# Row terms of the second layer over DRAM, tangent weights and shorter routing in a fused graph-attention and mixture-of-experts kernel

## The chip, the cores and the metric

The kernel runs on one core of a Trainium2 chip. A core has a matrix engine (TensorE, PE in the profile; its weight loads are listed apart as PEld), a vector engine (VectorE, DVE), an activation engine (ScalarE, ACT), a general engine (GpSimd, POOL) and a synchronisation engine (SyncE, SP) that in this kernel only issues transfers. Each engine executes its own list of instructions strictly in order, and the engines wait for one another through semaphores. Transfers between DRAM and the on-chip memory are issued from SP, ACT or POOL and carried by 16 DMA engines. The metric is the device time of one execution in microseconds.

## The reference

`x` is 64 batches of 256 rows of 256 floats, and `adj` is one 256 x 256 mask that all batches share. All arithmetic is float32. Two layers follow each other; cut to what matters:

```python
x = x + gat4(layernorm(x), adj)            # 4 heads of 64
x = x + layernorm(x) @ weight.T + bias
x = x + gat1(layernorm(x), adj)            # 1 head of 256, slope 0.01, then relu
x = x + moe(layernorm(x))                  # returns its tokens plus the experts' sum

# gat1: h = inp @ W; e[i, j] = leaky_relu(h[i] @ a1 + h[j] @ a2), -1e9 where adj == 0
#       softmax over j, times h
# moe:  logits = tokens @ router_w.T; probs = softmax(logits); the two largest of 8,
#       renormalised to a sum of 1; each expert is gelu(t @ w1 + b1) @ w2 + b2
```

Attention is computed per batch: every row `i` gets a term `h[i] @ a1`, every row `j` a term `h[j] @ a2`, and the score matrix is made from their sum. In the mixture each of the 16,384 tokens goes to two of the eight experts. With two weights that sum to one, a token's weights depend only on the difference `ed` of its second and first logit.

## The kernel before

**Attention.** One batch is 256 rows, two tiles of 128 rows (`NT = 2`). The exponential of a leaky ReLU of a sum is a maximum of two products of exponentials, so the kernel takes exponentials of the terms alone and builds a transposed score tile as `max(row term, bound) * masked factor` with one DVE instruction per tile of 128 x 256. The row terms, one number for each attention row, must then stand along the free dimension, the same on all 128 partitions.

There are two ways to bring them there. For the four heads of the first layer, `send_terms` (L535) turns them on DVE, SP (ACT before batch 18) writes them to a scratch in DRAM (L623), and a second transfer, `spread_terms` (L554, issued at L556), reads that scratch into every partition of the tile `z`. For the single head of the second layer, `scores1` (L522) lets PE do it: for each of the two row tiles a transpose of a broadcast column (L525) puts the terms into a PSUM bank `pd`, and the two instructions of L530 read them from there. `projected1` (L499) makes the exponentials `ex` on ACT (L513), the scaled values (L514) and the masked factor `me` (L519). `attended` (L578) multiplies scores and values (L586) and takes reciprocals of the row sums (L593).

**Routing.** The batches are routed in chunks: eleven of four batches, seven of two and three of one, 61 in all; the last three batches are computed dense, with all experts on all rows. `route` (L1079) finds the two best experts of every token (`top_two`, L783), counts tokens with two matmuls (L1105 and L1106), accumulates over the row tiles with a scan (L1116 for chunks of four; otherwise eight scans at L1122), and sends each row with its row number and weights to a position in the DRAM list `xs` by scattered transfers of POOL (`send`, L1059, issued at L1061). The weights come from the exponential of `ed` on ACT (L1112) and four DVE instructions (`two_weights`, L810). `route_dense` (L1190) does the same for a dense batch, with its exponential at L1195.

**Experts.** The list is worked off in "pairs" of 256 rows of one expert. `expert_pair` (L877) loads rows and first-layer weights (L893, L904, L922), `hidden` (L951) and `result` (L977) multiply, and `scatter` (L985) adds the 256 results to the output with two transfers of POOL that add in DRAM (L991). Each pair's two adds wait until the two adds of the pair before have landed, as different pairs can hold the same output row. The last routed chunk fills up partly filled pairs with filling rows (L1171) whose weights give zero. A filling row needs an output row to be added to: `fill` (L303 to L309) names rows of the last batch, `B - 1`.

That batch is dense, and its own output is a plain store. `store_dense` (L1030) therefore holds the store of batch 63 back until every scatter has been issued, and makes it wait for the last two adds. At the start, `fill_spare` (L313) stores zeros to the output rows of that batch, and the first scatter waits for it.

**Order.** Python generators stand for jobs. In each step of a loop (from L1242) the active jobs run in order of the rank they yielded last; a positive rank ends a job's share of the step, a negative one only re-sorts it inside the step. A batch starts every third step (`TICKS = 3`). What the generators call in this order is the order of the instructions on each engine; the loop knows no durations. `batch_layers` (L596) is a batch's job.

Of the kernel before, what the change touches and what calls it, by code (L numbers as in the profile page):

```python
# [9 lines left out]
F32 = mybir.dt.float32  # L10
# [5 lines left out]
P = 128  # L16
# [11 lines left out]
def kernel(  # L28
# [251 lines left out]
    def pack_expert(e):  # L280
# [22 lines left out]
    fill = const.tile([P, 2, ROW], F32, tag="fill", name="fill")  # L303
    nc.gpsimd.memset(fill, 0.0)
    nc.gpsimd.iota(
        fill[:, :, D : D + 1].bitcast(I32), pattern=[[1, 2], [1, 1]], base=(B - 1) * N,
        channel_multiplier=2,
    )
    nc.vector.memset(fill[:, :, D + 1 : D + 2], -1.0)  # L309
# [3 lines left out]
    def fill_spare():  # L313
        nc.sync.dma_start(
            out=xs_d[E * CAP * PAIR :, :].rearrange("(p t) c -> p t c", t=2), in_=fill
        )
        d = nc.sync.dma_start(
            out=out_rows[(B - 1) * N :, :].rearrange("(p t) c -> p t c", t=2), in_=fill[:, :, :D]
        )
        tc.add_to_no_dep_group("out", d.ins)  # L320
        based.append(d.ins)
        yield 90

    def once(work):
# [30 lines left out]
    scan_mask = const.tile([P, E, NTC], F32, tag="scan_mask", name="scan_mask")  # L355
    nc.vector.memset(scan_mask, 1.0)
    nc.vector.memset(scan_mask[:, :, 0:1], 0.0)

# [163 lines left out]
    def scores1(ex, me):  # L522
        pd = bank("pd", [N])
        for t in range(NT):
            nc.tensor.transpose(  # L525
                pd[:, t * P : (t + 1) * P], ex[:, t, 1:2].to_broadcast([P, P]), ident
            )
        z = work.tile([P, NT, N], F32, tag="z1", name="z1", bufs=1)
        for j in range(NT):
            nc.vector.scalar_tensor_tensor(  # L530
                z[:, j, :], pd, ex[:, j, 2:3], me[:, j, :], op0=ALU.max, op1=ALU.mult
            )
        return [z[:, j, :] for j in range(NT)]

# [61 lines left out]
    def batch_layers(b, c0, xng, lg):  # L596
# [81 lines left out]
        xT = transposed(x2)  # L678
        yield 20
        q, ex, me = projected1(xT, rstd, b)  # L680
        yield 25
        z = scores1(ex, me)
        yield 40
        pvs, rinv = attended(
            q[:, :, None, :], 1, lambda j, h, t: z[j][:, t * P : (t + 1) * P]
# [97 lines left out]
    def top_two(c, nt, lg, first):  # L783


        rt = lambda shape, name: chunk_tile(shape, name, c)
        vec, tt = nc.vector, nc.vector.tensor_tensor
        emb = em8[:, None, :].to_broadcast([P, nt, E])
        ohs, tops, lcur = rt([2, nt, E], "ohs"), [], lg
        for k in range(2):  # L790
            top = rt([nt], f"top{k}")
            vec.tensor_reduce(top, lcur, AX.X, ALU.max)
            eq = rt([nt, E], "eq")
            tt(eq, lcur, top[:, :, None].to_broadcast([P, nt, E]), ALU.is_equal)
# [12 lines left out]
        tt(ed, tops[1], tops[0], ALU.subtract)  # L807
        yield ohs, ed

    def two_weights(less, second, ed):  # L810

        nc.vector.tensor_scalar(less, ed, 1.0, None, op0=ALU.add)
        nc.vector.reciprocal(less, less)
        nc.vector.tensor_tensor(second, ed, less, ALU.mult)
        nc.vector.tensor_tensor(less, less, second, ALU.subtract)

    rows = [keep.tile([P, E], F32, tag="rows", name="rows")]  # L820
    nc.vector.tensor_scalar(rows[0], region, float(PAIR), None, op0=ALU.mult)
# [208 lines left out]
    def store_dense(b):  # L1030

        own = dense_batch[b]
        yield 99
        while b == B - 1 and (scatters or len(added) < 2 * PAIRS):
            yield 99
        d = nc.sync.dma_start(
            out=out_rows[b * N : (b + 1) * N, :].rearrange("(t p) d -> p t d", p=P),
            in_=own["base"],
        )
        before = added[-2:] + based if b == B - 1 else []  # L1040
        tc.declare_no_dep(
            d.ins, query=SYNC, group="out", keep=before,
            reason="no row is added to here, or every add is in their chain",
        )
        for ins in before:
            tc.add_manual_dep(d.ins, ins.name, AFTER, reason="filling rows were added here")
        tc.add_to_no_dep_group("out", d.ins)
        nc.sync.nop()

# [29 lines left out]
    def route(c, row0, nt, n, last, xng, lg):  # L1079
# [29 lines left out]
        both = rt([2, E, nt], "both")  # L1109
        vec.tensor_copy(both, pp)  # L1110
        pre, tot = both[:, 0], both[:, 1]
        nc.scalar.activation(ed, ed, AF.Exp)  # L1112
        tt(tot[:, :, 0], tot[:, :, 0], rows[0], ALU.add)
        run = rt([E, nt], "run")
        if nt == NTC:
            vec.tensor_tensor_scan(  # L1116
                run.rearrange("p e t -> p (e t)"), scan_mask.rearrange("p e t -> p (e t)"),
                tot.rearrange("p e t -> p (e t)"), 0.0, ALU.mult, ALU.add,
            )
        else:  # L1120
            for e in range(E):
                vec.tensor_tensor_scan(  # L1122
                    run[:, e, :], ones[:, :nt], tot[:, e, :], 0.0, ALU.mult, ALU.add
                )
        rows[0] = run[:, :, nt - 1]
        tt(pre, pre, run, ALU.add)
        if spread:
# [8 lines left out]
        vec.tensor_copy(pos, posf)  # L1136
        if not spread:
            yield from later(90, 1, 2)
        two_weights(tail[:, :, 1], tail[:, :, 2], ed)
        for i, xe in enumerate(xng):  # L1140
            vec.tensor_copy(xe[:, :, D + 1 :], tail[:, i * NT : (i + 1) * NT, :])
        parts = allot(c, n, False)
# [69 lines left out]
    PAIRS = ROUTED * NT + E - 1  # L1212

    def jobs():
        b = done = taken = 0
# [104 lines left out]
```

## Time and profile before

The three timed runs gave 1497.18, 1497.51 and 1500.99 us. The profile is of another execution, which took 1509.41 us.

| quantity | value |
|---|---|
| median of three runs | 1497.51 us |
| profiled execution | 1509.41 us, span 1507.6 us |
| PE busy, weight loads busy | 1429.0 us (95%), 1263.9 us (84%) |
| DVE busy | 1252.7 us (83%) |
| ACT busy | 1024.6 us (68%) |
| POOL busy | 870.2 us (58%) |
| transpose of row terms, second layer (L525) | 128, 278 ns mean |
| scores, second layer (L530) | 128, 460 ns mean |
| activation table loads, all lines | 130, 1283 ns each |
| adds to the output (L991) | 258, 1605 ns mean, idle before them 206.6 us |

A group's row gives source line, engine, operation, output and inputs, count, busy time, mean duration of one, and the engine's idle time just before. Durations of matmuls overlap[...]: what a matmul takes from its successors is the distance between starts. The table-load count is the sum of the groups of that operation: 65 before the gelu of L961, 47 before L513, 8 before L1112, 6 before L647, 3 before L1195 and 1 at L235.

### The profile page before, as it was taken

How to read it: one execution, taken by the hardware profiler on the slowest of the kernel's cores; microseconds unless marked ns; L12 is line 12 of the kernel's file. 1: busy time of each engine (PE TensorE's matmuls, PEld its weight loads, DVE VectorE, ACT ScalarE, POOL GpSimd, SP SyncE). 2: the span in 40 equal slices, each digit the busy share in tenths (PEclk: the TensorE clock that was granted, in tenths of full speed). 3: DMA queues.
4: the chain of work that ended last, by engine and by line, in shares of the span. 5: the costliest groups of instructions: out<-in, count | busy, mean ns of one | idle time of the engine just before them, and what ended most of it. 6: DMA issues, size and time to landing. Idle time of an engine off the chain costs nothing. (4 is left out here: it accounts for less than half of the span.)

```text
span 1507.6 us, 30029 instructions
## 1 busy us (share of the span) xinstructions
PE 1429.0 (95%) x8138; PEld 1263.9 (84%) x8138; DVE 1252.7 (83%) x4476; ACT 1024.6 (68%) x2403; POOL 870.2 (58%) x845
## 2 busy tenths in 40 slices
PE   6899999999999999999999999999999999879996
PEld 5788888889898998988998989888888887658885
DVE  7699999888898888889898988998888888765543
ACT  1477667577777777777777787667777878764331
POOL 2122536355867576666758585776666667643444
PEclk9899999899999999999999999999999999999999
DMA  4732334556877777877877677768777775887843
GB/s 134 241 97 67 117 104 131 155 149 142 196 172 190 157 183 155 177 177 180 187 157 183 151 186 164 181 164 187 179 167 170 153 170 124 192 180 161 156 83 50
DMA packets 354354, 236.37 MB, mean 157 GB/s; under 512 B 246276, under 2 KB 316428, under 8 KB 354188
## 3 DMA queue, kind: packets, MB, share of 16 engines
q1 hardware_dynamic: 301272, 158.16, 41.3%
q0 software_dynamic: 48864, 66.33, 23.8%
q10 hardware_dynamic: 4052, 9.98, 2.2%
q8 instruction: 67, 1.10, 0.3%
q14 instruction: 99, 0.81, 0.2%
HBM read 146.00 MB, written 88.35 MB: 155 GB/s over the span
## 5 line engine op out<-in xcount | busy, mean ns | idle before, releaser
L991 POOL DMA_INDIRECT out_dram<-y,xt x258 | 414.1, 1605 | 206.6 <-issue 71.5
L586 PE MATMUL pv<-q,z 128*128 128x65 f32 (+1 forms) x2560 | 365.9, 298 | 0.4
L586 PEld LDWEIGHTS pv<-q,z 128*128 128x128 f32 x2560 | 333.0, 194 | 13.1 <-DVE z L572 1.1
L1061 POOL DMA_INDIRECT xs<-xng,pos x244 | 259.5, 1064 | 65.3 <-issue 60.3
L970 PE MATMUL py<-w2s,hT 128*128 (+1 forms) x1224 | 283.5, 382 | 11.5 <-ACT hT L961 10.3
L970 PEld LDWEIGHTS py<-w2s,hT 128*128 128x128 f32 x1224 | 229.1, 191 | 45.4 <-ACT hT L961 14.2
L955 PE MATMUL ph<-sT,we 128*128 128x256 f32 x1032 | 241.9, 383 | 4.5 <-DVE y L980 2.9
L572 DVE SCALAR_TENSOR_TENSOR z<-z,q,mask 128x256 f32<-128x256 f32 x504 | 231.6, 482 | 15.5 <-DMA z<-terms 6.6
L955 PEld LDWEIGHTS ph<-sT,we 128*128 128x128 f32 x1032 | 195.6, 192 | 32.4 <-DVE y L980 3.6
L461 ACT COPY xT<-pt 128x512 f32<-128x512 f32 x209 | 121.4, 588 | 105.0 <-PE pt L455 72.2
L948 ACT ACTIVATE y<-y,w 128x256 f32<-128x256 f32 x258 | 113.2, 498 | 115.3 <-DVE y L980 100.9
L961 ACT ACTIVATE hT<-ph,we 128x256 f32<-128x256 f32 x306 | 124.1, 472 | 63.5 <-PE ph L955 46.3
L408 POOL TENSOR_SCALAR rstd<-mv 128x4 f32<-128x4 f32 (+1 forms) x66 | 15.6, 236 | 239.4 <-DVE mv L381 184.4
L506 PE MATMUL pq<-wx,xT 128*128 128x259 f32 x512 | 128.8, 394 | 18.6 <-ACT xT L461 16.9
L426 ACT ACTIVATE off<-x,sums 128x256 f32<-128x256 f32 x256 | 129.3, 505 | 8.4 <-DVE x L669 1.6
L506 PEld LDWEIGHTS pq<-wx,xT 128*128 128x128 f32 x512 | 95.6, 193 | 42.6 <-ACT xT L461 25.6
L471 PE MATMUL pq<-wx,xT 128*128 128x268 f32 x512 | 127.1, 391 | 2.8 <-DVE xT L117 1.6
L980 DVE TENSOR_TENSOR y<-py,b2s 128x512 f32<-128x512 f32 x129 | 85.7, 685 | 50.0 <-PE py L970 37.3
L662 PE MATMUL pf<-wfT,xT 128*128 128x256 f32 x512 | 123.8, 385 | 0.0
L471 PEld LDWEIGHTS pq<-wx,xT 128*128 128x128 f32 x512 | 97.5, 191 | 21.9 <-DVE xT L117 1.8
L690 ACT ACTIVATE rel<-pv,rinv 128x256 f32<-128x256 f32 x128 | 54.0, 469 | 76.4 <-DVE rinv L593 52.2
L662 PEld LDWEIGHTS pf<-wfT,xT 128*128 128x128 f32 x512 | 94.7, 195 | 10.8
(174 smaller groups left out, 2400.8 us busy)
## 6 DMA issues: line engine op xcount, KB each, us to landing
we<-wpack SPq DMA_DIRECT2D x145, 288.0 KB
xr<-xs SPq DMA_DIRECT2D x516, 64.0 KB
z<-terms SPq DMA_DIRECT2D x46, 512.0 KB
xin<-in_x_dram SPq DMA_DIRECT2D x64, 256.0 KB
out_dram<-base SPq DMA_DIRECT2D x61, 256.0 KB
xblk<-in_x_dram SPq DMA_DIRECT2D x188, 64.0 KB
z<-terms ACTq DMA_DIRECT2D x17, 512.0 KB
out_dram<-y,xt POOLq DMA_INDIRECT x258
```

What stands on the lines that cost most here:

```text
L426: nc.scalar.activation(off, src[:, t, :], AF.Square, bias=sums[:, t : t + 1], scale=-float(D), accum_out=sq[:, at + t : at + t + 1],)
L461: nc.scalar.copy(dst, pt)
L471: nc.tensor.matmul(pq.rearrange("p h c -> p (h c)"), xT[:, k, t * P : (t + 1) * P], wx[:, k, :], start=(k == 0), stop=(k == KT - 1),)
L506: nc.tensor.matmul(pq, xT[:, k, t * P : (t + 1) * P], wx1[:, k, :], start=(k == 0), stop=(k == KT - 1),)
L572: nc.vector.scalar_tensor_tensor(z[:, j, :, h, :], terms, q[:, j, h, HD + 2 : HD + 3], masks[0][:, j, :].rearrange("p (t i) -> p t i", t=N ...
L586: nc.tensor.matmul(pv[:, h, :], z(j, h, t), q[:, j, h, : d + 1], start=(j == 0), stop=(j == NT - 1),)
L662: nc.tensor.matmul(pf[:, t, :], xT[:, k, t * P : (t + 1) * P], wfT[:, k, :], start=(k == 0), stop=(k == KT - 1),)
L955: nc.tensor.matmul(ph[:, f, :], we[:, k * D + f * P : k * D + (f + 1) * P], xT[:, k, :], start=(k == 0), stop=(k == KT - 1),)
L961: nc.scalar.activation(hT[:, f, :], ph[:, f, :], AF.Gelu, bias=we[:, C_B1 + f : C_B1 + f + 1])
L970: nc.tensor.matmul(py[:, t, :], hT[:, f, t * P : (t + 1) * P], w2s[:, e, f * D : (f + 1) * D].rearrange("p e c -> p (e c)"), start=(f == 0 ...
L991: d = nc.gpsimd.indirect_dma_start(out=out_rows, out_offset=bass.IndirectOffsetOnAxis(ap=xt[:, t, 0:1].bitcast(I32), axis=0), in_=y[:, t, ...
L1061: d = nc.gpsimd.indirect_dma_start(out=xs_d[: E * CAP * PAIR, :], out_offset=bass.IndirectOffsetOnAxis(ap=at, axis=0), in_=xe, in_offset=None,
```

## The change

There are four edits, and one that follows from them.

Firstly, from batch 18 on (`SETTLED`), the second layer's row terms go over DRAM as those of the first layer do. `send_terms1` writes 256 numbers with a transfer from SP; a second one, after the first has landed, reads them into all partitions of the part of `z1` that the last score instruction writes. The transposes and the PSUM bank are left out there. `z1` is allocated before that transfer, and has one buffer as before.

Secondly, the two weights are written with a tangent: their difference is `tanh(-ed / 2)`, and the second is half of one minus it. One ACT instruction and one DVE instruction take the place of one and four. The chunk's activation uses `Tanh` where it used `Exp`.

Thirdly, chunks of one batch and the dense batches find their two experts with the eight-maximum instruction and its index instruction, one of each for each row tile, and chunks of one and two batches use one masked scan in place of eight. Their masks are set on POOL at the start.

Fourthly, filling rows name the rows of the first batch. The zeros at the start and the hold on the last batch's store are left out.

```diff
-        fill[:, :, D : D + 1].bitcast(I32), pattern=[[1, 2], [1, 1]], base=(B - 1) * N,
+        fill[:, :, D : D + 1].bitcast(I32), pattern=[[1, 2], [1, 1]], base=0,
...
-        d = nc.sync.dma_start(
-            out=out_rows[(B - 1) * N :, :].rearrange("(p t) c -> p t c", t=2), in_=fill[:, :, :D]
-        )
-        tc.add_to_no_dep_group("out", d.ins)
-        based.append(d.ins)
...
+    def send_terms1(ex, b):
+
+        ud = tc.dram_tile([N], F32, name=f"terms1_{b}")
+        nc.sync.dma_start(out=ud.rearrange("(t p) -> p t", p=P), in_=ex[:, :, 1])
+        return ud
+
+    def scores1(ex, me, z, spread):
+
+        terms = z[:, NT - 1, :]
+        if not spread:
+            terms = bank("pd", [N])
+            for t in range(NT):
+                nc.tensor.transpose(
+                    terms[:, t * P : (t + 1) * P], ex[:, t, 1:2].to_broadcast([P, P]), ident
+                )
         for j in range(NT):
             nc.vector.scalar_tensor_tensor(
-                z[:, j, :], pd, ex[:, j, 2:3], me[:, j, :], op0=ALU.max, op1=ALU.mult
+                z[:, j, :], terms, ex[:, j, 2:3], me[:, j, :], op0=ALU.max, op1=ALU.mult
             )
...
-        yield 25
-        z = scores1(ex, me)
+        spread = b >= SETTLED
+        if spread:
+            yield -22
+            ud = send_terms1(ex, b)
+            yield -52
+        z = work.tile([P, NT, N], F32, tag="z1", name="z1", bufs=1)
+        if spread:
+            nc.sync.dma_start(out=z[:, NT - 1, :], in_=rows_to_all(ud, N))
+        yield 45 if spread else 25
+        z = scores1(ex, me, z, spread)
...
+        if nt == NT:
+            yield top_two_of_few(c, nt, lg, first)
+            return
...
-    def two_weights(less, second, ed):
-
-        nc.vector.tensor_scalar(less, ed, 1.0, None, op0=ALU.add)
-        nc.vector.reciprocal(less, less)
-        nc.vector.tensor_tensor(second, ed, less, ALU.mult)
-        nc.vector.tensor_tensor(less, less, second, ALU.subtract)
+    def top_two_of_few(c, nt, lg, first):
+
+        top = chunk_tile([nt, E], "eq", c)
+        at = chunk_tile([nt, E], "l2", c, dt=mybir.dt.uint32)
+        for t in range(nt):
+            nc.vector.max(top[:, t, :], lg[:, t, :])
+            nc.vector.max_index(at[:, t, :], top[:, t, :], lg[:, t, :])
+        ohs = chunk_tile([2, nt, E], "ohs", c)
+        for k in range(2):
+            nc.vector.tensor_tensor(
+                ohs[:, k], jrow[:, None, :E].to_broadcast([P, nt, E]),
+                at[:, :, k : k + 1].to_broadcast([P, nt, E]), ALU.is_equal,
+            )
+        nc.vector.tensor_scalar(first, at[:, :, 0], float(-E), None, op0=ALU.add)
+        ed = chunk_tile([nt], "ed", c)
+        nc.vector.tensor_tensor(ed, top[:, :, 1], top[:, :, 0], ALU.subtract)
+        return ohs, ed
+
+    def second_weight(second, less):
+
+        nc.vector.tensor_scalar(second, less, -0.5, 0.5, op0=ALU.mult, op1=ALU.add)
...
-        while b == B - 1 and (scatters or len(added) < 2 * PAIRS):
-            yield 99
...
-        before = added[-2:] + based if b == B - 1 else []
...
-        nc.scalar.activation(ed, ed, AF.Exp)
+        nc.scalar.activation(tail[:, :, 1], ed, AF.Tanh, scale=-0.5)
...
-        if nt == NTC:
-            vec.tensor_tensor_scan(
-                run.rearrange("p e t -> p (e t)"), scan_mask.rearrange("p e t -> p (e t)"),
-                tot.rearrange("p e t -> p (e t)"), 0.0, ALU.mult, ALU.add,
-            )
-        else:
-            for e in range(E):
-                vec.tensor_tensor_scan(
-                    run[:, e, :], ones[:, :nt], tot[:, e, :], 0.0, ALU.mult, ALU.add
-                )
+        vec.tensor_tensor_scan(
+            run.rearrange("p e t -> p (e t)"), scan_masks[nt].rearrange("p e t -> p (e t)"),
+            tot.rearrange("p e t -> p (e t)"), 0.0, ALU.mult, ALU.add,
+        )
...
-        two_weights(tail[:, :, 1], tail[:, :, 2], ed)
+        second_weight(tail[:, :, 2], tail[:, :, 1])
...
-        nc.scalar.activation(ed, ed, AF.Exp)
         two = chunk_tile([2, NT], "two", c)
-        two_weights(two[:, 0], two[:, 1], ed)
+        nc.scalar.activation(two[:, 0], ed, AF.Tanh, scale=-0.5)
+        second_weight(two[:, 1], two[:, 0])
```

More of the change, by code (lines that the diff above doesn't have):

```diff
@@ L354 @@
     region = iota([E], [[CAP, E]], 0, 0, "region")
-    scan_mask = const.tile([P, E, NTC], F32, tag="scan_mask", name="scan_mask")
-    nc.vector.memset(scan_mask, 1.0)
-    nc.vector.memset(scan_mask[:, :, 0:1], 0.0)
+    scan_masks = {}
+    for nt in sorted({nb * NT for nb in CHUNKS}):
+        m = const.tile([P, E, nt], F32, tag=f"scan_mask{nt}", name=f"scan_mask{nt}")
+        nc.gpsimd.memset(m, 1.0)
+        nc.gpsimd.memset(m[:, :, 0:1], 0.0)
+        scan_masks[nt] = m
     half_done = []
@@ L520, in projected1 @@
         return q, ex, me
[L522 to L526, printed above, removed]
-            )
-        z = work.tile([P, NT, N], F32, tag="z1", name="z1", bufs=1)
+    def send_terms1(ex, b):
[10 more added lines that the diff above has]
+                )
         for j in range(NT):
             nc.vector.scalar_tensor_tensor(
-                z[:, j, :], pd, ex[:, j, 2:3], me[:, j, :], op0=ALU.max, op1=ALU.mult
+                z[:, j, :], terms, ex[:, j, 2:3], me[:, j, :], op0=ALU.max, op1=ALU.mult
             )
@@ L1039, in store_dense @@
         )
-        before = added[-2:] + based if b == B - 1 else []
-        tc.declare_no_dep(
-            d.ins, query=SYNC, group="out", keep=before,
-            reason="no row is added to here, or every add is in their chain",
-        )
-        for ins in before:
-            tc.add_manual_dep(d.ins, ins.name, AFTER, reason="filling rows were added here")
+        tc.declare_no_dep(d.ins, query=SYNC, group="out", reason="no row is added to here")
         tc.add_to_no_dep_group("out", d.ins)
@@ L1111, in route @@
         pre, tot = both[:, 0], both[:, 1]
-        nc.scalar.activation(ed, ed, AF.Exp)
+        nc.scalar.activation(tail[:, :, 1], ed, AF.Tanh, scale=-0.5)
         tt(tot[:, :, 0], tot[:, :, 0], rows[0], ALU.add)
         run = rt([E, nt], "run")
-        if nt == NTC:
-            vec.tensor_tensor_scan(
-                run.rearrange("p e t -> p (e t)"), scan_mask.rearrange("p e t -> p (e t)"),
-                tot.rearrange("p e t -> p (e t)"), 0.0, ALU.mult, ALU.add,
-            )
-        else:
-            for e in range(E):
-                vec.tensor_tensor_scan(
-                    run[:, e, :], ones[:, :nt], tot[:, e, :], 0.0, ALU.mult, ALU.add
-                )
+        vec.tensor_tensor_scan(
+            run.rearrange("p e t -> p (e t)"), scan_masks[nt].rearrange("p e t -> p (e t)"),
+            tot.rearrange("p e t -> p (e t)"), 0.0, ALU.mult, ALU.add,
+        )
         rows[0] = run[:, :, nt - 1]
@@ L1211 @@
     FLUSH = 2 * (E - 1)
-    PAIRS = ROUTED * NT + E - 1
     def jobs():
```

## The prediction

> **What bounds the kernel now.** I read the page first, then stages, then one period in order of time, then the end. The stage view gives, for each stretch, an engine's busy us and its instructions, the granted clock, the DMA share and GB/s:
>
> ```profile
> 320.00:920.00 600.00, 594.20 (x3508) 534.01 (x3507) 532.65 (x1827) 455.45 (x1075) 406.50 (x381) 1.00 0.76 173
> 920.00:1200.00 280.00, 269.32 (x1543) 238.59 (x1541) 250.83 (x944) 209.03 (x470) 184.45 (x174) 0.99 0.77 172
> 1200.00:1320.00 120.00, 106.80 (x556) 91.39 (x556) 96.12 (x453) 95.93 (x201) 82.89 (x75) 0.96 0.73 157
> 1320.00:1507.60 187.60, 165.73 (x760) 141.27 (x758) 97.83 (x285) 73.87 (x164) 81.41 (x55) 0.99 0.66 125
> ```
>
> From 320 to 920 PE is busy 99% and its weight loads 89% of the time. PE's order of time in one period shows what a transpose costs:
>
> ```profile
> 493.23 3.62 PE L970 MATMUL py<-w2s,hT 128*128 x16
> 496.68 0.38 PE L525 MATMUL pd<-ident,ex 128*128 128x128 f32 x2
> 496.90 3.69 PE L586 MATMUL pv<-q,z 128*128 128x65 f32 x32
> 500.42 0.67 PE L455 MATMUL pt<-ident,xng 128*128 128x128 f32 x4
> ```
>
> No row has an idle time before it. The two transposes start at 496.68 and the next group at 496.90: 0.22 us for two, against 278 ns each in the groups, since ends overlap. So PE sets the pace here, at starts.
>
> After about 1200 another chain takes over. POOL's waits from 1210 to 1500:
>
> ```profile
> POOL out_dram L991 <- DMA out_dram<-y,xt: 32.1, 9, 6.2
> POOL out_dram L991 <- issue: 25.4, 41, 4.5
> POOL out_dram L991 <- ACT y L948: 16.4, 9, 4.7
> ...
> POOL rstd L446 <- ACT off L426: 1.1, 1, 1.1
> ```
>
> There is next to no wait for other engines' results left but those of L991; from 300 to 900 POOL waited 83.1 us for L381 and 43.2 us for L426. Of the releasers named before L991, y was long done: the last pair's y ended at 1476.7, and its add started at 1497.86. What POOL waits for is the landing of the adds before. At the end (POOL's order of time, then SP's):
>
> ```profile
> 1490.85 1.56 POOL L991 DMA_INDIRECT out_dram<-y,xt  x1 [2.92 <-DMA out_dram<-y,xt]
> 1492.71 1.56 POOL L991 DMA_INDIRECT out_dram<-y,xt  x1 [0.30 <-issue]
> 1497.86 1.56 POOL L991 DMA_INDIRECT out_dram<-y,xt  x1 [3.59 <-issue]
> 1499.72 1.56 POOL L991 DMA_INDIRECT out_dram<-y,xt  x1 [0.30 <-issue]
> ```
>
> ```profile
> 1495.96 8.17 SPq L1036 DMA_DIRECT2D out_dram<-dbase  x2
> ```
>
> A pair takes 1.86 us from first to second add, 1.56 us for the second, about 3 us to land: 6.4 us. The second store of L1036 waits for the last landing: the row of SP ends at 1504.13, the store's issue takes 0.40, so it began at 1503.7, and the span ends 3.9 us later.
>
> [...] the first layer's terms, issued at 495.19, let the dependent read go at 497.60, 2.4 us later. [...] L572 takes 482 ns from SBUF, 468 from PSUM[...].
>
> **The change, part by part.** The sum is made against the profiled execution, 1509.41 us, 12 us above the median; I take the same difference off the median.
>
> *Transposes.* Batches 18 to 63 lose two each, 92 in all, 46 x 0.22 = 10.1 us of PE time. Up to batch 58 (its scores are near 1186 us) PE is the pace: 41 batches x 0.22 = 9.0 us. The other 1.1 us fall where POOL's adds are the pace: nothing there.
>
> *What takes their place.* Two transfers on SP per batch. In the built order the write stands before L623, the read after the load of L96 and before L556. SP's waits from 300 to 900:
>
> ```profile
> SPq L623 <- DVE stats L380: 219.0, 29, 9.1
> SPq L556 <- DMA terms<-ut: 25.4, 29, 1.7
> ```
>
> SP stands idle 7.6 us before each L623, so two issues of 0.35 to 0.55 us cost nothing, but delay what follows by that, and only if the write has not landed. In the period above, batch 26's `ex` is ready at 492.69. The write can land 2.4 us later, 495.1; SP then has L623 until 495.72 and L96 until 496.22, and issues the read at 496.3. Behind it on SP stand L556, the store of L736 and the pairs' loads; L556 waits until 497.60 anyway, so none is delayed unless the write lands 2 us later than this. The read queues behind the 256 KB of L96: at 173 GB/s (stage view) 1.5 us, its own 128 KB 0.75 us. Estimates for its landing: 2.4 us after issue, 498.7, at the low end; 2.4 + 1.5 + 0.75, 501.0, at the high end. DVE wants it here:
>
> ```profile
> 500.19 0.83 DVE L530 SCALAR_TENSOR_TENSOR z<-pd,ex,me 128x256 f32<-128x256 f32 x2
> 500.94 0.17 DVE L593 RECIPROCAL rinv<-pv 128x4 f32<-128x4 f32 x1
> 502.27 0.18 DVE L593 RECIPROCAL rinv<-pv 128x4 f32<-128x4 f32 x1 [1.15 <-PE pt L455]
> ```
>
> I take 499.7, in time; and up to 1.15 us of delay would go into the wait before 502.27. Queued behind a late L530 are those reciprocals, then L641, for which ACT's exponential waits. Between batches 52 and 56, where L530 follows `ex` after 5.9 us (batch 53) and not 7.5 (batch 26), I charge 0.2 us each: +1.0 us. The score instruction reads SBUF: [...] +0.014 (L572) on DVE, hidden by PE. 46 x 129 KB are 2.5% more bytes. The delay of `z`'s 512 KB read, at most 0.75 us, meets a reserve: it is issued at 497.60, and L572 starts near 508.6.
>
> *Weights.* Four DVE operations of L812 to L815, 3.5 + 4.0 + 3.5 + 3.6 us over 21 chunks, become one (about 3.9): -10.7 us of DVE. *Scans.* 80 scans, 6.7 us busy, become 10 of up to 0.32: -3.5. *Top two.* Six times, 12 operations near 0.18 us become 8, of which 4 are unknown: from 0.1 us (a small memset) to 0.5 (two and a half reduces of 0.19), so +0.6 to -1.0 us each. All of it is work that PE's 99% hides in the first long stage; only in 920 to 1200, where PE idles 11 us, may shorter routing count: seven chunks of two lose 0.9 us of DVE each, 6.3 us; I take a tenth, -0.6, between 0 and -4. *Masks.* Six small memsets on POOL at the start, about 0.1 us each, ahead of the first norms: up to 0.6 us, I take 0.3. *Table loads.* In the built order 14 of 130 vanish, all after batch 61's `ex` (1255 us), as the tangent lies in a table that is loaded already: 18.0 us of ACT. In that stage the adds are the pace, so I take nothing; if they are not, PE's idle time there is the prize: 13 + 22 us in the last two stages by busy time.
>
> *Filling rows and the end.* The store of batch 63 no longer waits for the adds. The last L1023 ends at 1500.27; store and end take 3.9 us: 1504.2, against 1503.7 for the last landing. So 1507.6 - 1504.2 = -3.4 us. The zeros at the start (0.67 us of SP issue at 74.04) are hidden. The adds themselves stay 258.
>
> Sum: -9.0 + 1.0 - 0.6 + 0.3 - 3.4 = -11.7 us: 1497.7 for the profiled execution, 1486 for the median.
>
> **Rivals.** *The tables count too.* The adds' chain is released only when the last rows have been sent, and hT, with a table load before it, stands in the way. For: PE's idle time above, and a table load of 1.28 us in the chain of waits at 1370. Against: y waits 20 us for its add. It would give 10 us more, 1476. *Only the end counts.* PE's freed slot is filled by waits, because DVE (89% busy) or ACT, with their fixed orders, pace the batch. For: DVE's share. Against: no idle time on PE. It gives 1497.5 - 3.4 = 1494. *The read comes late* (slower). If the 128 KB land more than 1.15 us after DVE wants them in most batches, DVE stops, and PE behind it. From 0.25 us of stall that reaches PE per batch (11.7 / 46) the gain is gone; at 0.6 us it is 27.6 - 11.7 = +16, 1513. For: a DMA share of 0.76 and the load ahead of it. Against: the estimates above. *The change does nothing*: excluded for the transposes, which are gone from the built order.
>
> **How the numbers follow.** Chances: mine 0.58, tables 0.18, only the end 0.15, late read 0.09. What can be told from no change is 0.3%, 4.5 us. Mine and the tables are faster, 0.76; of "only the end" a fifth is too, with a late routing gain: 0.79 faster. The rest of it, and one hundredth of the late read, is the same: 0.13. Slower 0.08. The range goes from the tables' 1476 to 1495, past "only the end", and leaves out the late read.
>
> **What would show it.** Right: L525 has 36 rows left, the distance of batches in 320 to 920 falls by about 0.2 us, L530's successor waits less than 0.2 us a batch for its transfer, L1036 issues right behind L1023. Wrong: a row "DVE z <- DMA z<-terms" of over 10 us, or idle time on PE where there is none now.

## The result, and the profile after

The changed kernel takes 1811.80 us (1807.61 to 1822.95, six runs) against 1497.35 us (1496.77 to 1503.31, six runs) before: a ratio of 1.2097, 95% interval 1.206 to 1.2134. It is 21% slower, where 1486 us and a small gain had been forecast. Its profiled execution spans 1809.2 us.

The costliest groups of the changed kernel (columns as before: line, engine, operation, count, busy us, mean ns, idle time before and its releaser). L592 is the product of scores and values, L536 the score instruction of the second layer, L453 the transposes of the normalised rows:

```profile
L592 PE MATMUL pv<-q,z 128*128 128x65 f32 (+1 forms) x2560 | 415.1, 321 | 5.2 <-DVE z L536 4.8
...
L536 DVE SCALAR_TENSOR_TENSOR z<-z,ex,me 128x256 f32<-128x256 f32 x92 | 44.6, 484 | 337.4 <-DMA z<-terms 335.5
L453 PE MATMUL pt<-ident,x 128*128 128x128 f32 x512 | 101.4, 323 | 196.0 <-DVE x L675 196.0
```

The score instruction itself costs what it did (484 ns against 460). In front of it stands a wait of 335.5 us; in the kernel before, VectorE stood idle 0.0 us ahead of this instruction. The waits of the whole execution (engine, line and what it waited for; then total us, times, longest) show what stands behind it:

```profile
DVE z L536 <- DMA z<-terms: 335.5, 46, 13.1
ACT e L653 <- DVE hp L647: 277.8, 47, 10.1
...
PEld pt L453 <- DVE x L675: 209.2, 82, 11.0
...
PE pt L453 <- DVE x L675: 196.0, 56, 10.6
```

All 46 batches wait, 7.3 us each. VectorE stops; what follows the scores on it (L647) comes late for ScalarE, and x of L675 comes late for the transposes of TensorE. These waits follow one another and do not add up: the 335.5 us are the origin. The transfer queue of SP shows why the terms are late:

```profile
SPq L523 <- ACT q L512: 268.0, 46, 13.3
SPq L694 <- DMA terms<-ex: 251.1, 45, 11.0
SPq L629 <- DVE stats L378: 124.2, 45, 11.4
```

L523 is the new write, L694 the new read. The read waits 5.6 us per batch for the write of 1 KB to land (251.1 / 45), after SP has already issued L629 and the load L96 in between. One period in order of time on SP (start us, duration us, issue), then on VectorE (in brackets the idle time before the row), then on TensorE:

```profile
512.51 0.38 SPq L523 DMA_DIRECT2D terms<-ex  x1
515.00 0.55 SPq L629 DMA_DIRECT2D terms<-ut  x1
515.59 0.44 SPq L96 DMA_DIRECT2D xin<-in_x_dram  x1
521.13 0.34 SPq L694 DMA_DIRECT2D z<-terms  x1
522.67 0.34 SPq L562 DMA_DIRECT2D z<-terms  x1
```

```profile
519.05 1.31 DVE L117 STREAM_TRANSPOSE sT<-xr 128x512 f32<-128x512 f32 x2
526.69 1.00 DVE L536 SCALAR_TENSOR_TENSOR z<-z,ex,me 128x256 f32<-128x256 f32 x2 [6.33 <-DMA z<-terms]
```

```profile
529.74 1.11 PE L453 MATMUL pt<-ident,x 128*128 128x128 f32 x4 [3.35 <-DVE x L675]
530.65 3.63 PE L592 MATMUL pv<-q,z 128*128 128x257 f32 x8
```

The write is issued at 512.51, the read only at 521.13, 8.62 us later, and its data are there 5.56 us after that. Over the 46 batches the medians are 9.2 us (7.4 to 11.6) from write to read, and 5.2 us from read to scores. The forecast had 2.4 and 3.4. VectorE is free at 520.36 and stands until 526.69.

The stages, cut at the `ex` of batches 18, 47 and 63 (columns: us, busy us and instructions of PE, PEld, DVE, ACT, POOL, then the granted clock, which is the share of its full speed at which TensorE ran, the DMA share and GB/s):

```profile
323.00:1102.00 779.00, 650.18 (x3404) 563.97 (x3402) 525.08 (x1772) 447.92 (x1052) 404.44 (x376) 0.89 0.74 136
1102.00:1599.00 497.00, 393.48 (x1999) 342.00 (x1998) 324.13 (x1223) 283.61 (x638) 259.23 (x240) 0.87 0.70 130
1599.00:1809.00 210.00, 183.68 (x826) 156.63 (x824) 106.45 (x333) 76.76 (x182) 90.66 (x62) 0.95 0.71 134
```

In the profile of before the same stages took 590, 381 and 206 us at clocks of 1.00, 0.99 and 0.98. That execution was about 12 us above the median. Of nine later profiles of kernels that still transpose on TensorE and have no slow write, seven took 581 us for the first of the three stages; the other two, of one comparison in which the kernel before was slower too (1504 us), took 588 and 591. I take 581 as the base. The first two stages carry the loss: 198 us over 29 batches (189 against the profile of before) and 116 over 16, about 7 us per batch, near the wait of L536. TensorE is busy 83% and no longer 99% of the first stage, its granted clock there falls to 0.89, and the matmuls of L592 take 507 ns where those of L586 took 385 in the same shape (257 columns). Of the 198 us, 129 are idle time of TensorE (779.00 - 650.18) and about 69 are longer busy time (650.18 against 581.00 in no_terms_third, shown below). The last stage, where the pairs' adds are the pace, is nearly as it was.

### The profile page after: what moved, and what is told of

The parts are those of the page before. It is cut to its first block, busy times and chain, and to the rows that moved or that the text cites. A ratio compares the mean times of both kernels' runs of the same rounds, so it can differ in the third digit from the quotient of the medians.

```text
span 1809.2 us, 29837 instructions
## 1 busy us (share of the span) xinstructions
PE 1524.5 (84%) x8046; PEld 1324.9 (73%) x8046; DVE 1238.6 (68%) x4320; ACT 1008.7 (56%) x2389; POOL 876.1 (48%) x851
## 5 line engine op out<-in xcount | busy, mean ns | idle before, releaser
L592 PE MATMUL pv<-q,z 128*128 128x65 f32 (+1 forms) x2560 | 415.1, 321 | 5.2 <-DVE z L536 4.8
L592 PEld LDWEIGHTS pv<-q,z 128*128 128x128 f32 x2560 | 367.7, 207 | 32.2 <-issue 4.8
L536 DVE SCALAR_TENSOR_TENSOR z<-z,ex,me 128x256 f32<-128x256 f32 x92 | 44.6, 484 | 337.4 <-DMA z<-terms 335.5
L453 PE MATMUL pt<-ident,x 128*128 128x128 f32 x512 | 101.4, 323 | 196.0 <-DVE x L675 196.0
L984 PE MATMUL ph<-sT,we 128*128 128x256 f32 x1032 | 251.9, 395 | 3.9 <-DVE y L1009 2.1
L453 PEld LDWEIGHTS pt<-ident,x 128*128 128x128 f32 x512 | 65.1, 159 | 220.9 <-DVE x L675 209.2
L653 ACT ACTIVATE e<-hp 128x512 f32<-128x512 f32 x64 | 40.4, 631 | 301.2 <-DVE hp L647 277.8
L504 PE MATMUL pq<-wx,xT 128*128 128x259 f32 x512 | 144.6, 431 | 46.0 <-ACT xT L459 45.9
L504 PEld LDWEIGHTS pq<-wx,xT 128*128 128x128 f32 x512 | 103.9, 211 | 82.0 <-ACT xT L459 65.8
L444 POOL TENSOR_SCALAR rstd<-sq 128x4 f32<-128x4 f32 (+1 forms) x63 | 22.9, 364 | 220.0 <-ACT off L424 219.1
```

What stands on the lines that cost most here:

```text
L453: nc.tensor.transpose(pt[:, k, t * P : (t + 1) * P], by_block(src[:, t, :])[:, k] if blocks else src[:, t, k * P : (k + 1) * P], ident,)
L504: nc.tensor.matmul(pq, xT[:, k, t * P : (t + 1) * P], wx1[:, k, :], start=(k == 0), stop=(k == KT - 1),)
L592: nc.tensor.matmul(pv[:, h, :], z(j, h, t), q[:, j, h, : d + 1], start=(j == 0), stop=(j == NT - 1),)
L984: nc.tensor.matmul(ph[:, f, :], we[:, k * D + f * P : k * D + (f + 1) * P], xT[:, k, :], start=(k == 0), stop=(k == KT - 1),)
```

## The experiments

The theory after reading the traces: the write in 256 single numbers lands late, the read is late with it, and VectorE stops. There are three rivals: the read itself is what is late, behind the 256 KB of L96; or the mere presence of the new transfers slows the others; or another part of the change does it. A ratio is always to the kernel before, in the same comparison.

**no_terms: the rest of the change without the way over DRAM.**

```diff
-        spread = b >= SETTLED
+        spread = False
```

> The changed kernel with the transposes of the second layer's row terms back in all batches, and everything else of the change kept. Theory (the way over DRAM alone costs the time): 1494 us, 3.4 us below the kernel before from the end, or down to 1484 if the 14 table loads count. Rival (another edit, such as the filling rows or the routing, carries the loss): above 1700 us.

It ran at 1485.31 us, ratio 0.9927 (0.9898 to 0.9956) from four runs. In two later comparisons, on other chips, it came to 0.9984 (0.9966 to 1.0003) and 0.9938 (0.9917 to 0.9958). So the whole loss belongs to the terms' way over DRAM, and what is left of the change gains between 0.2 and 0.7% (the interval of the second comparison takes in no gain).

**rows_write: the same way, with the terms turned first.** One 128 x 32 transpose of VectorE puts them into rows, and the write has 8 pieces of 128 bytes instead of 256 of 4. `exs` are two fixed tiles of 128 x 2 x 16 that take the place of `ex1`.

```diff
+        ut = small.tile([P, S], F32, tag="ut1", name="ut1", bufs=1)
+        nc.vector.transpose(ut, exs[b % len(exs)].rearrange("p t c -> p (t c)"))
...
-        nc.sync.dma_start(out=ud.rearrange("(t p) -> p t", p=P), in_=ex[:, :, 1])
+        nc.sync.dma_start(
+            out=ud.rearrange("(t g r) -> g t r", t=NT, g=G), in_=ut[1 : P : S // NT, :]
+        )
```

> The changed kernel, but the 256 row terms are turned on DVE first (one 128x32 transpose, about 0.21 us a batch) and written to DRAM as 8 rows of 128 bytes, not as 256 pieces of 4 bytes. Theory (pieces of 4 bytes land late, the rest of the way is quick): from the write's issue to the read's issue about 3.6 us, not 9.2, and the time that was predicted, 1486 us (1480 to 1495). Rival (two more transfers in SP's list and on its queue are too many, whatever their pieces): above 1650 us. Between the two, 1500 to 1600 us, if the read also lands too late by itself.

1508.67 us, ratio 1.0089 (1.0062 to 1.0115). Some 300 of the 314 us are gone with the form of the write alone; the read, the bytes, the order on SP and the load ahead are the same. The read now goes 2.66 us after the write (median), mostly as soon as SP has issued the load. The expected 1480 to 1495 us were missed. The wait of the score instruction (L546 here) in the waits of rows_write:

```profile
DVE z L546 <- DMA z<-terms: 35.6, 37, 3.0
```

About 1 us in each of 37 batches remains. That is a late read of the kind that the forecast had as a rival.

**write_unread: the kernel before with the write alone.** Nobody reads it; the transposes stay.

```diff
+        if b >= SETTLED:
+            yield -22
+            ud = tc.dram_tile([N], F32, name=f"terms1_{b}")
+            nc.sync.dma_start(out=ud.rearrange("(t p) -> p t", p=P), in_=ex[:, :, 1])
```

> The kernel before with the 4-byte write of the row terms added from batch 18 on; nothing reads it, the transposes stay. Theory (only what waits for the landing loses): 1497 us, within 1%. Rival (the small pieces hold up the DMA engines, so that every transfer behind them is late): above 1550 us, and the 256 KB load right behind the write takes 6 us to move, not under 2.

1572.13 us, ratio 1.0523 (1.047 to 1.0577). So the write of 1 KB, which no instruction waits for, costs 5% by itself: it holds up other transfers. The 256 KB load of L96, issued behind it, has moved its 256 packets of 1 KB 7.5 us after its issue (median of batches between 330 and 1100 us, read from the packets of the trace), against 2.6 us in the kernel before. This answers the second rival in part, and called for two more experiments.

**probe: the time that a write takes to land, by its form.** The kernel before, with one write per batch from 18 on in six forms in turn, and right behind it a small read of the same place, so that the distance of the two issues is the landing.

```diff
+        kind = (b - SETTLED) % 6
+        got = small.tile([1, 1], F32, tag="got", name="got", bufs=2)
+        if kind == 0:
+            ud = tc.dram_tile([N], F32, name=f"probe_{b}")
+            nc.sync.dma_start(out=ud.rearrange("(t p) -> p t", p=P), in_=ex[:, :, 1])
+            nc.sync.dma_start(out=got, in_=ud[0:1][:, None])
+        elif kind == 1:
+            ud = tc.dram_tile([N, 16], F32, name=f"probe_{b}")
+            nc.sync.dma_start(
+                out=ud.rearrange("(t p) c -> p t c", p=P)[:, :, 0], in_=ex[:, :, 1]
+            )
+            nc.sync.dma_start(out=got, in_=ud[0:1, 0:1])
...
```

> The kernel before with one more write from SP per batch from batch 18 on, in six kinds in turn, each followed at once by a read of its first element, so that SP's gap between the two issues is the write's landing. Kinds: 256 pieces of 4 bytes side by side (as in the change), the same 64 bytes apart, the same 512 bytes apart, 256 pieces of 64 bytes, 256 of 512 bytes, 8 of 128 bytes. Theory A[...]: 9 us for the first kind, under 3 us for all others. Theory B (every piece below some size is slow wherever it lies): 9 us for the first three and more than 3 for 64 bytes, 2.4 for the last two. Theory C (the number of pieces counts): the same for the first five, and less for 8 pieces. The time itself says little, as SP waits inside every batch.

Medians of the distance from write to read, each form in seven or eight batches:

| form of the write | us to the read |
|---|---|
| 256 pieces of 4 B, adjacent | 8.32 (6.9 to 10.2) |
| 256 pieces of 4 B, 64 B apart | 2.88 |
| 256 pieces of 4 B, 512 B apart | 2.32 |
| 256 pieces of 64 B, adjacent | 2.52 |
| 256 pieces of 512 B, adjacent | 3.11 |
| 8 pieces of 128 B, adjacent | 2.38 |

SP's waits for these reads in the trace (L541 after the adjacent pieces of 4 B; L547 with 64 B between; L553 with 512 B between; L565 after pieces of 512 B):

```profile
SPq L541 <- DMA probe<-ex: 62.2, 8, 9.7
SPq L547 <- DMA probe<-ex: 20.7, 8, 4.1
SPq L565 <- DMA probe<-me: 17.6, 7, 3.3
SPq L553 <- DMA probe<-ex: 17.5, 8, 4.2
```

It is neither the number of pieces nor their size: 256 pieces of 4 B with gaps land about as fast as 8 rows of 128 B. It is that pieces of 4 B lie next to each other; distances between 4 and 64 B were not tried. The packets of this trace narrow it further. The adjacent write is recorded as 256 packets of 4 B, all of them through 1.1 to 2.6 us after its issue, and the read goes only 4.3 to 9.0 us after the last of them; after pieces of 64 or 512 B it goes at most 0.9 us after the last. So the time passes after the DMA engines have sent the pieces, before the write counts as landed.

**write_apart: write_unread with the pieces 64 B apart.**

```diff
-            ud = tc.dram_tile([N], F32, name=f"terms1_{b}")
-            nc.sync.dma_start(out=ud.rearrange("(t p) -> p t", p=P), in_=ex[:, :, 1])
+            ud = tc.dram_tile([N, 16], F32, name=f"terms1_{b}")
+            nc.sync.dma_start(
+                out=ud.rearrange("(t p) c -> p t c", p=P)[:, :, 0], in_=ex[:, :, 1]
+            )
```

> The kernel before with the unread 4-byte write of the row terms added, as in the run that took 1572 us, but with the 256 pieces 64 bytes apart. Same number and size of pieces, same queue. Theory[...]: within 1% of the kernel before, 1495 to 1510 us. Rival (the number of small pieces holds up the engines): about 1570 us as before.

1498.37 us, ratio 1.0019 (1.0003 to 1.0035). 5.2% become 0.2% with the same count and size of pieces. What had been held up shows in SP's waits between 320 and 1350 us, first of write_unread, then of write_apart: L556 waits there for the first layer's own terms, which are written after the unread ones.

```profile
SPq L556 <- DMA terms<-ut: 275.6, 42, 8.9
SPq L623 <- DVE stats L380: 75.1, 39, 2.9
```

```profile
SPq L556 <- DMA terms<-ut: 41.1, 43, 2.4
```

6.6 us per batch against 1.0. The first layer's write in rows, which lands in about 2.4 us, takes 5.6 us longer by these waits when adjacent 4-byte pieces went ahead of it, and what stands behind L556 on SP waits with it.

**rows_early: rows_write with the read right behind its write,** ahead of the first layer's write and the 256 KB of L96.

```diff
             ud = send_terms1(ex, b)
-            yield -52
+            yield -23
```

> The version that writes 8 rows of 128 bytes, with its read moved up in SP's list: directly behind its write, ahead of the first layer's write and of the 256 KB load of the next input. That version is at 1508.7 us with DVE waiting 35.6 us for the read (37 times), the changed kernel with the transposes back at 1485.3. Theory (what is left of the loss is the read's place behind the load; PE is the pace): DVE waits under 10 us, and 1475 to 1480 us, about 10 below the version with transposes, as 92 transposes of 0.11 us are gone. Rival 1 (PE's freed slot is worth nothing because DVE or ACT pace a batch): 1485 us. Rival 2 (any such transfer in the pairs' traffic is late): 1500 us or more.

1489.78 us, ratio 0.9962 (0.9948 to 0.9976), 19 us below rows_write. That is above the 1475 to 1480 us expected, and by the ratios no clear gain over no_terms. From write to read it takes 2.26 us, from read to scores 3.94 (4.29 in rows_write). What is left of the wait:

```profile
DVE z L546 <- DMA z<-terms: 8.5, 8, 2.7
```

The stage from batch 18 to 47 took 575 us, 6 less than the 581 of kernels that transpose on TensorE: 0.21 us for each of 29 batches. The following one did not gain (383 us against 374 in no_terms, though one profile each; in later profiles no_terms took 379 and 376 us there, so part of this difference can be chance).

**rows_mid: rows_early for batches 18 to 47 alone.**

```diff
-        spread = b >= SETTLED
+        spread = SETTLED <= b < 48
```

> rows_early with the terms sent over DRAM only for batches 18 to 47; from 48 on PE transposes again, as in no_terms. Stage theory: the transposes are worth 0.2 us per batch only where PE sets the pace (6 us between ex of batch 18 and of 47 there), and the extra transfers cost time only in the later stage, where rows_early took 383 us from batch 47 to 63 against 374 in no_terms. Then both gains add: 18 to 47 in about 575 us, 47 to 63 in about 374, a ratio near 0.9885 (about 1480 us) and about 0.4% below no_terms in this comparison. Rival, the adds: what is gained before batch 48 is waited out again before the adds of the pairs, so the ratio is that of no_terms, 0.9927. Second rival: the 0.2 us per batch was not due to the transposes but to chance of one profile; then 18 to 47 takes 581 us.

Beside it ran no_terms again:

> no_terms once more (the transposes back for every batch, the rest of the change kept), beside rows_mid and route_only in one comparison. Expected 0.9927 within its interval of 0.9898 to 0.9956, in all theories; it gives the base that rows_mid and route_only are held against.

rows_mid came to 0.9939 (0.9918 to 0.9961), no_terms_again to 0.9984 (0.9966 to 1.0003). The step between them is as expected, but both lie 0.5% above where they were put. Their first stages took 584 and 591 us, 6.6 apart, and not 575 and 581. In one more comparison:

> rows_mid once more, in one comparison with no_terms_third. The stage theory: 0.4% below no_terms_third, as in the comparison before (0.9939 against 0.9984), from the 0.2 us per batch in batches 18 to 47. Rival: the same ratio within 0.15%, the transposes' time being waited out before the adds.

> no_terms a third time, beside tanh_again. The two earlier comparisons differ, 0.9927 from few runs and 0.9984. If weights and routing add (0.45% and 0.2%): 0.9935. If the second comparison holds: 0.998.

rows_mid_again 1481.51 us, 0.9903 (0.9879 to 0.9927); no_terms_third 1488.42 us, 0.9938 (0.9917 to 0.9958). The quotient of the two is 0.9965 here and 0.9955 there; the intervals of each pair overlap, but the step came twice. The stages of rows_mid_again, then of no_terms_third, cut as above:

```profile
321.00:896.00 575.00, 575.00 (x3402) 521.42 (x3401) 526.96 (x1802) 446.87 (x1053) 397.83 (x376) 1.00 0.81 184
896.00:1273.00 377.00, 360.17 (x2029) 318.58 (x2027) 322.48 (x1222) 282.34 (x635) 255.67 (x237) 0.98 0.76 168
1273.00:1480.00 207.00, 180.51 (x832) 154.87 (x830) 107.18 (x334) 77.46 (x185) 94.38 (x66) 0.96 0.68 134
```

```profile
322.00:903.00 581.00, 581.00 (x3456) 526.32 (x3456) 520.16 (x1773) 446.30 (x1053) 393.70 (x376) 1.00 0.77 176
903.00:1279.00 376.00, 361.07 (x2037) 319.00 (x2036) 322.84 (x1222) 282.85 (x636) 254.37 (x235) 0.98 0.76 167
1279.00:1486.00 207.00, 178.52 (x828) 153.15 (x826) 107.59 (x336) 77.34 (x185) 95.24 (x67) 0.96 0.68 135
```

The 6 us of the first stage reach the end in this pair, because the other two stages are equal within 1 us. In the pair before, single profiles do not show it: rows_mid was 8 us longer in the second stage (387 against 379), and the two profiled executions ended together, though the medians are 6 us apart. As rows_mid took 387 and 378 us there without any of the new transfers, whether these cost time after batch 48 stays open. rows_mid is faster than the kernel before and the changed one: 0.6 and 1.0% below the kernel before in the two comparisons, of which some 0.4% are the transposes and the rest is what no_terms gains.

**fill_only: the filling rows alone,** in the kernel before.

```diff
-        fill[:, :, D : D + 1].bitcast(I32), pattern=[[1, 2], [1, 1]], base=(B - 1) * N,
+        fill[:, :, D : D + 1].bitcast(I32), pattern=[[1, 2], [1, 1]], base=0,
...
-        while b == B - 1 and (scatters or len(added) < 2 * PAIRS):
-            yield 99
...
-        before = added[-2:] + based if b == B - 1 else []
```

> The kernel before with the filling rows in the first batch alone: no zeros at the start, no hold on the last store. Prediction's step: -3.4 us, 1491 against 1494.7. Rival (the end is set by the adds' landing anyway, and more follows than their landing): under 1 us.

1496.49 us, 1.0008 (0.9993 to 1.0023): no gain. The last stores on SP in fill_only end 7 us before the span does:

```profile
1485.37 4.74 SPq L1029 DMA_DIRECT2D out_dram<-dbase  x2
```

What ends the program is on POOL's sequencer. The rows of its closing instructions (durations in ns least/median/greatest, then first and last start), first in the kernel before, then in fill_only:

```profile
L1315 POOLq DRAIN  x3: 46/113/8733, 1498.1 to 1507.4; - x3
```

```profile
L1302 POOLq DRAIN  x3: 46/113/8764, 1487.6 to 1496.9; - x3
```

The long one is recorded from just after the start of the next-to-last add (1497.86 and 1487.33) and takes 8.7 us in both kernels; the last add, 1.86 us later, falls within it, so how much of it is its own is not known. The span ends 9.7 and 9.8 us after that start, and between 9.4 and 9.8 us in all 17 profiles of this document, wherever the last store stood. The store of the last batch had room within it: in the kernel before, SP comes to its own closing DRAIN at 1506.2, and POOL's long one ends at 1506.8.

**tanh_only, tables_back: the weights.** tanh_only is the kernel before with the second edit alone. It has 116 table loads for 130, none of them in front of a tangent, and one VectorE instruction for four in each chunk. tables_back is tanh_only with an exponential in front of each tangent.

```diff
+        nc.scalar.activation(tail[:, :, 1], ed, AF.Exp)
         nc.scalar.activation(tail[:, :, 1], ed, AF.Tanh, scale=-0.5)
```

> The kernel before with the tangent weights alone; the built list has 116 table loads in place of 130. Prediction's step (loads are hidden behind the adds' chain, and DVE's shorter lists behind PE): within 1 us of before. Rival (the tables count too): 6 to 10 us faster, as the version of the change without its transfers was 9 to 11 us faster and the end explains 3.4.

> tanh_only with one more exponential of the same values in front of each tangent (overwritten by it), so that the 14 table loads come back while the four vector operations stay one. It tells whether the 0.45% of tanh_only is the table loads' or the vector operations'. If the loads': the ratio goes back to 1.000 (the activation added is about 0.2 us, 21 times, 4 us of ScalarE at most, so up to 1.002). If the vector operations': it stays at 0.9955 to 0.998.

> tanh_only once more beside tables_back. If the tables count by 6.7 us: 0.9955. If that was chance, or belongs to one chip alone as the two comparisons of no_terms (0.9927 and 0.9984) suggest: 0.998 to 1.0.

tanh_only 0.9955 (0.994 to 0.997); then, in one comparison, tanh_again 0.9968 (0.9949 to 0.9987) and tables_back 0.9969 (0.9944 to 0.9995). The table loads are back in tables_back (groups of that operation):

```profile
L955 ACT ACT_TABLE_LOAD x65 | 83.4, 1283 | 1.1
...
L1106 ACT ACT_TABLE_LOAD x8 | 10.3, 1283 | 0.1
```

Their 18 us of ScalarE, and the activations added, change nothing within the 0.3% that this pair of intervals can tell. tables_back has all 130 loads and still gains 0.3%: what it has less of is work on VectorE. That the loads add a part below 0.3% is not excluded.

**route_only: the third edit alone.**

> The kernel before with the third edit alone: the eight-maximum and its index in chunks of one batch and the dense batches, one masked scan for eight, masks set on POOL. no_terms gained 0.73%, tanh_only 0.45%, fill_only nothing. If the parts add, this gives 0.28%, a ratio of 0.997 (about -4 us, against the -0.6 + 0.3 us of the prediction). If the prediction's size is right: 0.9998, and the gain of no_terms is the weights' and more than tanh_only alone shows. If the parts overlap, since both shorten the same chain from the logits to the rows sent, it gives up to 0.5% alone.

1501.95 us against 1504.04, ratio 0.9981 (0.9965 to 0.9997): about 2 us, with an interval from next to nothing to 5.

## Why the prediction was wrong

**The step that failed** is, under "What takes their place", "The write can land 2.4 us later". The 2.4 us came from the first layer's terms, 32 rows of 128 B. The new write moves a quarter of the bytes, but as 256 numbers of 4 B side by side, and in that form it takes 8.3 us in the probe and 9.2 in the changed kernel. The forecast counted issues and bytes of the new transfers and never the pieces. The step said that none of the transfers behind it is delayed unless the write lands 2 us later than assumed; it landed 7 us later, so everything that the sentence names as queued behind the read on SP was late too. In place of a reserve of 1.15 us there was a wait of 7.3 us per batch, and the row "DVE z <- DMA z<-terms", named as the sign of being wrong above 10 us, came to 335.5.

**The second transfer's estimate** was also short: 3.4 us taken as likely (499.7 after an issue at 496.3), 4.7 at the high end. From the read's issue to the scores it is 5.2 us in the changed kernel, 4.3 with the write in rows, 3.9 with the read ahead of the load; in the last, VectorE waits for the read in 8 batches alone, so there it mostly lands sooner than that. With the write mended, this alone kept the kernel 0.9% slower (rows_write), and the order on SP decides it (rows_early). The forecast's bounds, 2.4 to 4.7 us, take in the 4.3 of the mended write, not the 5.2.

**Traffic.** "46 x 129 KB are 2.5% more bytes" priced the transfers for others by bytes. The write alone cost 5.2% (write_unread), almost all of it because the pieces touch (0.2% in write_apart).

**The rival "the read comes late"** had the place right: VectorE stops at L536, the successor of L530, and TensorE behind it. The stall that it priced, 0.6 us per batch, was twelve times too small. Its 0.09 chance rested on the same 2.4 us. Per batch, the loss is near the wait of L536; how much of it the lower granted clock adds was not measured apart, and the 69 us of longer busy time in the first stage are the figure for it that the stages give. By the clock records of the trace the first stage of the changed kernel has 29 stretches at half speed, one per batch, 171 us in all, and its clock is 0.89. Each of them begins 1.3 to 4.5 us after the start of an idle gap of TensorE such as the 3.35 us ahead of L453; these gaps are 1.4 to 6.0 us long, 3.35 us in the median.

**Transposes: right per batch.** 0.22 us for two, read from starts, is 0.21 us in rows_early, and 0.23 and 0.21 in the two pairs of rows_mid and no_terms ((581 - 575) / 29 in the second). It was taken to hold to batch 58, 9.0 us in all; in rows_early the 6 us of the first stage are all that can be seen.

**Masks** (+0.3 us) and the +1.0 us for batches 52 to 56 were not measured apart.

**Score instruction from SBUF: as small as forecast.** 484 against 460 ns is +0.024 us, where up to +0.014 had been taken from L572 (482 ns from SBUF, 468 from PSUM).

**Table loads at nothing: right within 0.3%**, and the rival "the tables count too", which promised 10 us, falls: tables_back equals tanh_again. **Vector work at nothing: wrong.** The forecast laid the 10.7 us of the weights, the scans and the shorter top two under TensorE's 99%, and charged -0.6 us in all. The weights alone gave 4.5 us in one comparison and 6.7 in the other, routing about 2. Where in the kernel this falls, the profiles do not tell: stages of tanh_only and the kernel before differ by no more than two executions of one kernel do.

**The end: wrong.** -3.4 us became 0. The store that ended last was followed backwards, but POOL's closing step, which ended within the same microseconds, was not looked for; it ends last with the store or without. The sentence "store and end take 3.9 us" joined two things that run side by side.

**Without the write's form** the remaining sum was near: -9.0 + 1.0 - 0.6 + 0.3 - 3.4 = -11.7 us, against -5.6 for rows_early and between -9 and -17 for rows_mid. That is partly luck: the 3.4 us of the end are not there, and weights and routing, priced at 0.6 us, bring some 6 to 9 in their own runs.

## What to carry to other kernels

Before a transfer is priced by the nearest row of a profile, compare the form of both on the DRAM side: how many pieces, how large, and whether small pieces touch; a small write in single numbers that touch should be turned into rows on chip first (one 128 x 32 transpose here), or be given gaps (in the probe it lands in 8.3 us as it is, in 2.4 as rows and in 2.9 with 64 B between the starts). A transfer for which an engine waits belongs ahead of bulk loads on its queue (19 us between rows_write and rows_early). An edit on an engine that hides behind another can still bring some tenths of a per cent (0.3 to 0.5% by the weights alone), and an end that looks bound by one chain should be checked for a second that ends with it.

## What the runs showed of the hardware

- A write of 256 pieces of 4 B lands in 8.3 us when they are adjacent in DRAM, in 2.9 us at 64 B and 2.3 us at 512 B between their starts. The size alone doesn't explain it, as all three have 4 B pieces, and adjacent pieces of 64 B land in 2.5 us. The delay comes after the pieces have been sent (4.3 to 9.0 us from the last packet to the read). What happens in that time was not shown.
- Such a write delays what comes behind it: the wait for the first layer's terms grew from 1.0 to 6.6 us per batch, the 256 KB load behind it took 7.5 us in place of 2.6, and a kernel in which nobody reads the write lost 5.2%.
- POOL's sequencer has a closing step, recorded with 8.35 to 8.76 us, that begins just after the start of the next-to-last add. In all 17 profiles the span ended 9.4 to 9.8 us after that start, whatever the last store did.
- The granted clock of TensorE was 0.87 to 0.89 in long stages in which it waited for late scores and was busy 79 to 83% of the time (the first two of the changed kernel), and 0.98 to 1.00 in the same stages of rows_mid_again and no_terms_third, in which it was busy 96 to 100%. In the changed kernel's first stage the 0.89 are made of full speed and of 29 stretches at half speed, of 3.4, 6.8 or 10.2 us.
